# A lower rank for the third group in the tail, and four PSUM banks for each group

## The chip, the core and the metric

The kernel runs on one core of a Trainium2 chip. The metric is the time of the kernel on the device in microseconds, the median of several runs. The engines are TensorE (PE, the matrix engine), VectorE (DVE), ScalarE (ACT), GpSimd (POOL) and SyncE (SP, which here does nothing but start DMA transfers). All of them work through their own queue of instructions in the order in which the program puts them there, and wait for each other by semaphores.

## What is computed

Four layers work on a tensor x of 16 images, 32 channels and 128 by 128 pixels. Before each layer x is group-normalised, and its result is added to x.

```python
x = x + _L0_conv_ref(_gn(x), ...)   # a recurrent layer over the skewed rows, 128 steps
x = x + _L1_conv_ref(_gn(x), ...)   # a 3x3 layer of sums of absolute differences
x = x + _L2_conv_ref(_gn(x), ...)   # 2-D Hartley transform, 32x32 modes mixed over channels, and back
x = x + _L3_conv_ref(_gn(x), ...)   # five edge filters, each normalised, then a small U-net
```

The change concerns the end of the last two layers. Layer 2 transforms every image by two multiplications with a table of cosines and sines, keeps 32 by 32 modes, mixes the channels with one weight matrix for each mode, and transforms back. Layer 3 applies five edge filters with a mean and a variance for each image, and then this chain, in which every step needs all of the one before:

```python
y = conv3x3(y, conv1_w, conv1_b); y = maxpool2(y)      # 160 channels in, 128x128 pixels
y = conv3x3(y, conv2_w, conv2_b); y = maxpool2(y)      # 64x64
y = conv3x3(y, conv3_w, conv3_b); y = maxpool2(y)      # 32x32
y = conv3x3(y, conv4_w, conv4_b)                       # 16x16
y = deconv2x2(y, ...); y = conv3x3(y, conv5_w, ...)    # up to 32x32
y = deconv2x2(y, ...); y = conv3x3(y, conv6_w, ...)    # up to 64x64
y = deconv2x2(y, ...); y = conv3x3(y, conv7_w, ...)    # up to 128x128
return orig * y
```

## The kernel before

**Stages.** `stage0` computes layer 0 for all images. `rest` computes the other three. Its first part, `Differences.run`, computes layer 1 image by image, which takes most of the time; DVE and ACT form the differences, and PE sums them (L645). Layers 2 and 3 are computed by the class `After` for groups of four images: one image has 32 channels, so four fill the 128 partitions. There are four groups. While `Differences.run` works on the images of the next group, the work of a finished group is woven between its instructions. What is left when layer 1 has come to its last image is called the tail here: a part of the third group, and the whole fourth or last group, which needs the last image of layer 1.

**The stages of a group.** `forward` (L1028): loads `xh` of x2, transform by L1116, L1131 and L1088, a store of the modes to HBM and loads of them back in another layout; `mixing` with the weight tables `mix` (L1203); the result `z` goes through HBM. `back` (L1230): L1267 and L1312 transform back, DVE adds the result to x2 (L1290), takes its statistics (L1292) and SP stores x3. `statistics` (L1376): x3 comes in frames `xp` of 16 rows, ACT normalises them, and PE forms a Gram matrix of the frames (L1403), from which DVE gets the variances of the five filtered images (L1463) and with them one folded set of weights for conv1 (L1530, L1532). `conv1` (L1662): a small part for the left and right edges (L1693), then eight chunks of 16 rows, each 25 taps of 16 matmuls (L1721), with some more matmuls in the first and the last chunk (L1738). A chunk fills four PSUM accumulators, one for each image; DVE adds the edge parts (L1757) and takes the 2x2 maxima (L1645), and then DVE or ACT adds the bias and moves the result to its place (`spread`, L1656 and L1659). `small_layers` (L1544): conv2 to conv4 (L1568), and conv5 and conv6, each composed with its deconvolution (L902, L927). `last` (L1777): conv7 composed with its deconvolution, in eight rounds of four accumulators (L902, L927); after each round DVE scales the four (L1850) and multiplies them with x3 (L1813), and after each second round ACT adds the mean (L1823) and SP stores the output.

**The order of the work in the tail.** A `Weave` is a generator of a group's work. It yields after each small piece with the time that the piece is thought to take. `drain` (L453) runs two of them, one for what is left of the third group and one for the last group: it always steps the one whose own clock is behind. In this way the pieces of the two groups are traced in turns. The instructions of `stage0` and of layer 1 are pinned to the order in which they are traced (`keep_order`); those of the tail are not. There a scheduler at build time puts each engine's instructions in order: among those that are ready in its own model of the machine, it takes the one with the smallest priority number. This number comes from a counter, `tc.cur_priority`, which goes up as instructions are traced, so that before the change the priority is the order of tracing.

**Where the tiles lie.** PSUM has eight banks, and one accumulator is one bank. The pool `b_ps` with four banks belongs to groups 0 to 2 throughout. The pool `c_ps`, with the four banks that layer 1 leaves, belongs to the last group. An accumulator is taken by `acc` (L986):

```python
self.banks += 1
ps = self.spare if self.weave.alone and self.banks // 4 % 2 else self.ps
return ps.tile([128, 512], F32, name="acc")
```

`spare` of the last group is `b_ps`, and `alone` becomes true when the third group has ended: from then on the last group takes four accumulators from one pool and the next four from the other. In SBUF the third group's tiles are on the left, with two frames and two residual buffers `xr3` for `last`; the last group's are on the right, with four of each. `alone` has two more effects: `spread` then gives each second image to DVE and the others to ACT, whatever its caller asks for, and `last` plans its stores 4 us and not 14 us after ACT. `stretch` lengthens the planned waits of a weave.

Of the kernel before, what the change touches and what calls it, by code (L numbers as in the profile page):

```python
# [7 lines left out]
F32 = mybir.dt.float32  # L8
# [340 lines left out]
class Weave:  # L349
# [10 lines left out]
    def __init__(self, work):  # L360
        self.work, self.pending = work, None
        self.pe = self.dve = self.act = self.now = self.base = 0.0
        self.until = self.ready = 0.0
        self.draining = self.alone = False
        self.stretch = 1.0
        self.finished, self.count, self.put_off, self.for_act, self.ends = -1, 0, [], [], {}
# [42 lines left out]
    def step(self):  # L409
# [3 lines left out]
        if v is None:  # L413
            return None
        if v is SUMMED:
            wait = self.lag()
# [33 lines left out]
                self.pe = start + us * CLOCK  # L450


def drain(*weaves):  # L453

    live = list(weaves)
    for w in live:
        w.draining, w.stretch = True, 1.5
    while live:
        w = min(live, key=lambda w: w.now)
        us = w.step()  # L460
        w.now = max(w.now + (us or 0.0), w.until)
        w.due(float("inf") if us is None else w.now)
        if us is None:
            live.remove(w)
            for w in live:
                w.alone, w.stretch = True, 1.0


def keep_order(nc, tc, start):

    last = {}
    for i in nc.cur_bb.bb.instructions[start:]:
        if i.engine in last:
            tc.add_manual_dep(
                i,
                last[i.engine].name,
                mybir.DependencyInfo(mybir.DependencyClass.NoSync, mybir.DependencyReason.DATA),
                reason="order",
            )
        last[i.engine] = i  # L480
# [5 lines left out]
LATE = 1.5  # L486
SLACK, CLOCK = 3.0, 1.0
SUMMED = ("summed",)


def rest(nc, tc, cst, sel16, bias, m1, r1, a, d, out):


    with ExitStack() as ctx:
        sm = ctx.enter_context(tc.tile_pool(name="s1_sm", bufs=1))
        stat = sm.tile([128, B, 8, 6], F32, name="stat2")
        with tc.tile_pool(name="s1_ps0", bufs=2, space=PSUM) as ps:
            first = Differences(nc, sm, ps, cst, sel16, m1, r1, a["adder_w"], d, stat)
        bg = ctx.enter_context(tc.tile_pool(name="b_ps", bufs=4, space=PSUM))
        after = After(nc, tc, "left", sm, bg, cst, bias, a, d, stat, out)  # L500
        weave = after.weave = Weave(after.work(range(NG - 1)))
        start = len(nc.cur_bb.bb.instructions)
        with ExitStack() as front:
            first.run(tc, front, weave)
        keep_order(nc, tc, start)

        end = copy.copy(after)
        end.side, end.ps = "right", ctx.enter_context(tc.tile_pool(name="c_ps", bufs=4, space=PSUM))
        end.spare = bg

        end.buffers = {"t_x": 8, "xm": 8, "xw": 4, "t_w": 6, "t_r": 8, "frames": 4, "gm": 5, "e_v": 6, "l_x": 4}
        end.weave = Weave(end.work([NG - 1]))
        end.weave.now = end.weave.base = weave.now
        end.weave.finished = B - 1
        drain(weave, end.weave)


class Differences:
# [103 lines left out]
    def finish(self, b, half, acc, xr, **_):  # L622
        nc = self.nc
        v = [xr[k // 2][:, 512 * (k % 2) : 512 * (k % 2) + 512] for k in range(4)]
        for k in range(4):
            nc.vector.scalar_tensor_tensor(v[k], acc[k], self.sumw, v[k], ALU.subtract, ALU.add)
        for k in range(4):
            nc.vector.bn_stats(self.stat[:, b, 4 * half + k, :], v[k])

        def store():  # L630
            for i in range(2):
                by_rows(nc, xr[i], jc_rows(self.d["x2"], b, half, 8 * i, 8), True)
            if half:
                self.weave.finished = b

        start = max(self.weave.dve, self.weave.pe)
        self.weave.pe, self.weave.dve = start + 2.6, start + 5.6
        self.weave.later(max(self.weave.dve - self.weave.base, 0.0) + 0.5, store)

    def sums(self, acc, d, i, first, last):  # L640
        c = 1 if i % 3 == 1 else 0
        for k in range(4):
            for j in range(4):
                row = 16 * j + 4 * k
                self.nc.tensor.matmul(  # L645
                    acc[k][32 * j : 32 * j + 32, :],
                    self.sel16[:, i // 9, :],
                    d[:, row : row + 4, c : c + W],
                    start=first,
                    stop=last,  # L650
                )

    def linear(self, acc, q, tap):

        kh, kw = tap // 3, tap % 3
        for j in range(4):
            for k in range(4):
                rows = slice(32 * k, 32 * k + 32)
                row = 16 * j + 4 * k + kh
                self.nc.tensor.matmul(  # L660
                    acc[k][32 * j : 32 * j + 32, :],
                    self.sel16[rows, 8, :],
                    q[rows, row : row + 4, kw : kw + W],
                    start=False,
                    stop=False,
                )
        self.weave.pe = max(self.weave.pe, self.weave.now) + 0.45
# [110 lines left out]
def normalised(nc, pool, ps, weave, mv, n, avg, eps, out):  # L778
# [5 lines left out]
    nc.tensor.matmul(p[:, :n], avg, mean, start=True, stop=True)  # L784
    yield SUMMED
    nc.vector.tensor_copy(out[:, 0], p[:, :n])
# [6 lines left out]
    nc.tensor.matmul(p[:, :n], avg, v, start=True, stop=True)  # L793
    yield SUMMED
    nc.vector.tensor_copy(v, p[:, :n])
# [34 lines left out]
class Composed:  # L830
# [10 lines left out]
    def compose(self, pool, ps):  # L841
# [5 lines left out]
        for par in range(4):  # L847
            for tap in range(4):
# [6 lines left out]
                for i, (q, k) in enumerate(terms):  # L855
# [8 lines left out]
                    yield 0.4  # L864
        yield SUMMED
        t = pool.tile([128, 25, 32], F32, name="co_t")
# [9 lines left out]
        nc.vector.tensor_reduce(t[:, 24], w3.rearrange("p t o -> p o t"), AX.X, ALU.add)  # L876
        yield SUMMED
        nc.sync.dma_start(self.store, t.rearrange("p t o -> p (t o)"))
        p = ps.tile([128, 512], F32, name="acc")
        for j in range(4):  # L880
            nc.tensor.matmul(p[32 * j : 32 * j + 32, :1], t[:32, 24], self.bd[:32], start=True, stop=True)
        yield SUMMED
        nc.vector.tensor_add(self.bias, p[:, :1], self.b3)
# [72 lines left out]
class After:  # L956


    def __init__(self, nc, tc, side, sm, ps, cst, bias, a, d, stat, out):
        self.nc, self.tc, self.side, self.ps, self.cst, self.bias = nc, tc, side, ps, cst, bias  # L960
        self.a, self.d, self.stat, self.out = a, d, stat, out
        self.spare, self.banks = None, 0
        self.buffers = {"t_x": 4, "xm": 3, "xw": 2, "t_w": 3, "t_r": 4, "frames": 2, "gm": 3, "e_v": 3, "l_x": 2}
        store = [d["up"][i] for i in range(3)]
        self.up5 = Composed(nc, sm, a, "deconv1", "conv5", bias[:, 7:8], bias[:, 4:5], store[0])
        self.up6 = Composed(nc, sm, a, "deconv2", "conv6", bias[:, 8:9], bias[:, 5:6], store[1])
        self.up7 = Composed(nc, sm, a, "deconv3", "conv7", bias[:, 9:10], bias[:, 6:7], store[2])
# [17 lines left out]

    def acc(self):  # L986

        self.banks += 1
        ps = self.spare if self.weave.alone and self.banks // 4 % 2 else self.ps
        return ps.tile([128, 512], F32, name="acc")  # L990

    def prepare(self):

# [998 lines left out]
def program(nc, tc, a, at, out):  # L1992
    def scratch(name, *shape):
        return nc.dram_tensor(name, shape, F32, kind="Internal").ap()

    d = {f"x{i}": scratch(f"x{i}_d", B, C, H, W) for i in (1, 2, 3)}
    d["q"] = nc.dram_tensor("q_d", (B, C, H + 2, W + 2), F16, kind="Internal").ap()
    d["xm"], d["z"] = (scratch(n, B, C, M1, M1) for n in ("xm_d", "z_d"))
    d["y6"] = scratch("y6_d", NG, 128, 66 * 66)
    d["fold"] = scratch("fold_d", 5, 128, 90 * 32)  # L2000
    d["up"] = scratch("up_d", 3, 128, 25 * 32)
    with tc.tile_pool(name="keep", bufs=1) as keep:
        cw = keep.tile(list(a["consts"].shape), F32, name="cw")
        nc.scalar.dma_start(cw, a["consts"])
        cst = {n: cw[:, lo:hi] for n, (lo, hi) in at.items()}
        sel16 = keep.tile([128, 9, 32], F16, name="sel16")
        nc.scalar.dma_start(sel16, a["sel16"])
        bias = keep.tile([128, 10], F32, name="bias")
        nc.scalar.dma_start(bias, a["bias"])

        m1, r1 = stage0(nc, tc, keep, cst, a["x"], a["xs"], a["w0"], a["b1"], a["b2"], d["x1"])
        rest(nc, tc, cst, sel16, bias, m1, r1, a, d, out)
# [17 lines left out]
```

## Time and profile before

| | us |
|---|---|
| median of 3 runs | 6794.93 |
| lowest and highest of them | 6793.73, 6800.52 |
| the profiled execution | 6791.52 |
| its span, first to last instruction | 6789.7 |
| PE busy in the span | 5402.1 (80%) |
| DVE busy | 5640.5 (83%) |
| ACT busy | 5537.1 (82%) |

The shares of the whole span belong to layer 1 and say little about the tail. The page shows the tail at the right end of the rows that cut the span into 40 slices: DVE and ACT fall from nine tenths to two or three, while PE stays at seven to nine.

```profile
PE   3697777787777879997877788999877774897896
DVE  7898999999999999989999999999999993224223
ACT  3898999999999999999999999999999991132222
PEclk9998999999999989998989899999889996997997
```

A digit is the busy share of one fortieth of the span (170 us) in tenths; in the row PEclk it is the clock that TensorE was granted, in tenths of the full speed. Line numbers in the profile are those of the kernel before; the changed kernel's lines lie up to three further down or up.

### The profile page before, as it was taken

The numbers are of one execution on the slowest core, as the hardware profiler recorded it, in microseconds if no ns is written. First come the engines' busy times: TensorE is split into PE (matmuls) and PEld (weight loads), VectorE is DVE, ScalarE is ACT, GpSimd is POOL, SyncE is SP. The second block draws the span as 40 slices with busy tenths as digits, with TensorE's granted clock in tenths as the row PEclk, the third lists the DMA queues.
The fourth block names the chain that finished last, engine by engine and source line by source line (L and its number), as shares of the span: only waits on it lengthen the run. The fifth ranks groups of instructions, "written<-read, shape, count | busy, mean of one in ns | idle before, by whom it ended". The sixth has DMA issues, their size and how long they took to land. (4 is left out here: it accounts for less than half of the span.)

```text
span 6789.7 us, 271989 instructions
## 1 busy us (share of the span) xinstructions
PE 5402.1 (80%) x127580; PEld 2816.8 (41%) x127580; DVE 5640.5 (83%) x6946; ACT 5537.1 (82%) x3419; POOL 90.9 (1%) x83
## 2 busy tenths in 40 slices
PE   3697777787777879997877788999877774897896
PEld 3575333333343433333334343333333343454564
DVE  7898999999999999989999999999999993224223
ACT  3898999999999999999999999999999991132222
POOL 0000000000000010000000000000000000000000
PEclk9998999999999989998989899999889996997997
DMA  7553312213343431312353443222264246342414
GB/s 316 201 189 126 77 49 63 60 30 71 80 127 108 113 109 46 85 44 59 86 152 92 145 117 79 56 57 51 61 139 120 66 135 194 99 149 72 92 42 104
DMA packets 381685, 689.12 MB, mean 101 GB/s; under 512 B 68048, under 2 KB 234448, under 8 KB 369680
## 3 DMA queue, kind: packets, MB, share of 16 engines
q1 hardware_dynamic: 373088, 637.30, 34.2%
q0 software_dynamic: 7040, 33.80, 1.5%
q8 instruction: 998, 16.35, 1.0%
q14 instruction: 127, 1.04, 0.1%
q10 hardware_dynamic: 432, 0.64, 0.0%
HBM read 507.28 MB, written 164.32 MB: 99 GB/s over the span
## 5 line engine op out<-in xcount | busy, mean ns | idle before, releaser
L755 ACT ACTIVATE d_act<-q,neg 128x8192 f16<-128x8192 f16 (+1 forms) x622 | 4404.3, 7148 | 138.0 <-PE acc L645 117.2
L758 DVE TENSOR_SCALAR d_dve<-q,qw 128x8192 f16<-128x8192 f16 (+1 forms) x1682 | 3878.9, 2363 | 163.5 <-PE acc L645 143.3
L645 PE MATMUL acc<-d_dve,sel 128*32 128x512 f16 x26912 | 1864.5, 400 | 475.4 <-DVE d_dve L758 412.2
L645 PEld LDWEIGHTS <-sel 128*32 128x32 f16 x36864 | 1014.3, 100 | 2122.4 <-issue 1455.1
L1721 PE MATMUL acc<-xp,wf 32*32 32x512 f32 x25600 | 1040.4, 616 | 57.4 <-issue 53.3
L645 PE MATMUL acc<-d_act,sel 128*32 128x512 f16 x9952 | 716.4, 408 | 329.6 <-ACT d_act L755 310.0
L1721 PEld LDWEIGHTS acc<-xp,wf 32*32 32x32 f32 x25600 | 416.1, 104 | 429.0 <-issue 345.8
L1659 ACT ACTIVATE y<-pooled,b 32x128 f32<-32x128 f32 x488 | 195.1, 400 | 389.1 <-DVE pooled L1645 382.4
L675 PE MATMUL acc<-q,zero 128*32 128x512 f16 x7088 | 509.2, 399 | 0.0
L902 PE MATMUL acc<-y,u_conv 32*32 32x256 f32 (+1 forms) x9728 | 373.8, 472 | 90.8 <-issue 63.7
L221 PE MATMUL pg<-h,wb 64*64 64x20 f32 (+15 forms) x8192 | 340.1, 303 | 61.5 <-DVE h L249 35.3
L235 ACT ACTIVATE gt<-pg,bias 128x20 f32<-128x20 f32 (+15 forms) x1024 | 332.5, 384 | 42.3 <-PE pg L221 40.4
L1362 ACT ACTIVATE xp<-xp,shift,stats 128x1280 f32<-128x1280 f32 (+1 forms) x128 | 182.6, 1434 | 185.8 <-DMA xp<-x_d 170.6
L221 PEld LDWEIGHTS pg<-h,wb 64*64 64x64 f32 x8192 | 250.1, 149 | 136.9 <-DVE h L249 82.5
L675 PEld LDWEIGHTS <-zero 128*32 128x32 f16 x7088 | 214.7, 101 | 195.7 <-issue 40.2
L1850 DVE TENSOR_SCALAR s<-acc,l_ms,l_one 128x512 f32<-128x512 f32 x128 | 102.1, 821 | 202.8 <-PE acc L902 202.8
L902 PEld LDWEIGHTS acc<-y,u_conv 32*32 32x32 f32 x9728 | 177.0, 111 | 216.4 <-issue 164.2
L1823 ACT ACTIVATE xr<-xr,l_ms 128x1024 f32<-128x1024 f32 x64 | 70.0, 1141 | 222.8 <-DVE xr L1813 222.8
L1403 PE MATMUL acc<-xp 32*64 32x204 f32 (+3 forms) x8576 | 238.6, 344 | 16.1 <-issue 15.6
L1403 PEld LDWEIGHTS acc<-xp 32*64 32x64 f32 (+1 forms) x8576 | 168.2, 135 | 108.9 <-issue 100.4
L221 PE MATMUL pg<-xn,wb 64*64 64x2 f32 (+63 forms) x4096 | 184.1, 289 | 28.6 <-issue 18.6
L1568 PE MATMUL acc<-y,w_conv 32*32 32x512 f32 (+2 forms) x4608 | 162.5, 497 | 28.4 <-issue 16.5
(218 smaller groups left out, 3711.9 us busy)
## 6 DMA issues: line engine op xcount, KB each, us to landing
xp<-x_d SPq DMA_DIRECT2D x112, 640.0 KB
q<-q_d SPq DMA_DIRECT2D x128, 536.2 KB
xr<-x_d SPq DMA_DIRECT2D x128, 512.0 KB
x_in<-in_x_dram SPq DMA_DIRECT2D x16, 2048.0 KB
xn<-in_xs_dram SPq DMA_DIRECT2D x64, 512.0 KB
res<-in_x_dram SPq DMA_DIRECT2D x64, 512.0 KB
x_d<-res SPq DMA_DIRECT2D x64, 512.0 KB
xq<-x_d SPq DMA_DIRECT2D x256, 128.0 KB
```

The lines of the kernel that those rows point to most:

```text
L221: nc.tensor.matmul(bank[c][q][64 * pair : 64 * pair + 64, :, :width], wb[half, 4 * kind + KIND[q]].rearrange("p b o -> p (b o)"), v[half], ...
L235: nc.scalar.activation(gt[:, q, :, :n], bank[c][q][:, :, :n], AF.Tanh if q == G else AF.Sigmoid, bias=bias[:, KIND[q] : KIND[q] + 1],)
L645: self.nc.tensor.matmul(acc[k][32 * j : 32 * j + 32, :], self.sel16[:, i // 9, :], d[:, row : row + 4, c : c + W], start=first, stop=last,)
L675: self.nc.tensor.matmul(acc[k][32 * j : 32 * j + 32, :], self.zero, q[:, :4, :W], start=False, stop=False)
L755: nc.scalar.activation(dst, src, AF.Relu, bias=self.neg[:, i : i + 1])
L758: nc.vector.tensor_scalar(dst, src, self.qw[:, i : i + 1], 0.0, ALU.subtract, ALU.max)
L902: nc.tensor.matmul(acc[blk][32 * j : 32 * j + 32, o : o + rows * n], t[part, 4 * par + tap, :], src[part, top : top + rows, left : left + ...
L1362: nc.scalar.activation(v, v, AF.Identity, bias=self.shift3, scale=self.stats3[:, 1])
L1403: nc.tensor.matmul(gram[blk][j : j + width, at : at + n], xp[part, l, 2 + j : 2 + j + width], xp[part, rows, j : j + width + 4], start=sta ...
L1568: nc.tensor.matmul(acc[blk][32 * j : 32 * j + 32, : rows * n], wc[name][part, tap, :], src[part, at : at + rows, kw : kw + n], start=tap == 0,
L1659: nc.scalar.activation(d, s, AF.Identity, bias=bj)
L1721: nc.tensor.matmul(acc[blk][32 * j : 32 * j + 32, :], tap_of("all", tap)[rows], xp[rows, 4 * j + kh : 4 * j + kh + 4, kw : kw + W], start= ...
```

## The change

```diff
-def drain(*weaves):
-
-    live = list(weaves)
-    for w in live:
-        w.draining, w.stretch = True, 1.5
+def drain(tc, *weaves):
+
+    live, turn = list(weaves), {}
+    for k, w in enumerate(live):
+        w.draining, w.alone, w.stretch = True, True, 1.5
+        turn[w] = tc.cur_priority + BEHIND * (len(live) - k)
     while live:
         w = min(live, key=lambda w: w.now)
+        tc.cur_priority = turn[w]
         us = w.step()
         w.now = max(w.now + (us or 0.0), w.until)
         w.due(float("inf") if us is None else w.now)
+        turn[w] = tc.cur_priority
         if us is None:
             live.remove(w)
-            for w in live:
-                w.alone, w.stretch = True, 1.0
+            for v in live:
+                v.stretch = 1.0
...
+BEHIND = 1000000
...
         end.side, end.ps = "right", ctx.enter_context(tc.tile_pool(name="c_ps", bufs=4, space=PSUM))
-        end.spare = bg
...
-        drain(weave, end.weave)
+        drain(tc, weave, end.weave)
...
-        self.spare, self.banks = None, 0
...
     def acc(self):
 
-        self.banks += 1
-        ps = self.spare if self.weave.alone and self.banks // 4 % 2 else self.ps
-        return ps.tile([128, 512], F32, name="acc")
+        return self.ps.tile([128, 512], F32, name="acc")
```

Each of the two weaves gets a counter of priorities of its own. The third group's (the first argument of `drain`) starts two million above the present value, the last group's one million above, so that every instruction of the last group in the tail has a smaller number than every one of the third. The weaves are still stepped by their clocks, so the tracing takes turns as before. Each group has its own four PSUM banks to the end. `alone` is true for both groups throughout the tail, and with it the division of `spread` between DVE and ACT; `stretch` becomes 1.0 for the group that is left when the other's tracing has ended.

## The prediction

> **What bounds the kernel now.** The change touches only the tail, so I first looked for where the tail begins. The view of the sums of stage 1 (L645) shows its last matmul at 5592.9 us; the span is 6789.7 us, so the tail is 1196.8 us. Then I cut the tail into stretches:
>
> ```profile
> core 0: us, PE busy (x) PEld busy (x) DVE busy (x) ACT busy (x) POOL busy (x), PEclk, DMA share, GB/s
> 5593.00:5740.00 147.00, 72.71 (x1746) 53.44 (x1738) 67.54 (x217) 27.14 (x43) 5.32 (x11) 0.72 0.75 221
> 5740.00:6253.00 513.00, 435.72 (x14185) 249.06 (x14186) 162.07 (x471) 117.79 (x248) 8.82 (x19) 0.89 0.36 107
> 6253.00:6519.00 266.00, 229.01 (x7194) 142.17 (x7192) 69.45 (x138) 69.80 (x129) 0.21 (x1) 0.94 0.38 87
> 6519.00:6592.60 73.60, 73.51 (x2363) 62.03 (x2367) 11.13 (x40) 6.40 (x16) 0.00 (x0) 1.00 0.02 4
> 6592.60:6636.00 43.40, 36.45 (x1153) 24.58 (x1146) 20.20 (x76) 13.29 (x36) 0.00 (x0) 0.87 0.11 29
> 6636.00:6703.00 67.00, 45.37 (x1207) 27.28 (x1207) 23.28 (x40) 17.14 (x29) 0.00 (x0) 0.65 0.62 134
> 6703.00:6770.70 67.70, 46.83 (x2027) 33.04 (x2027) 33.70 (x49) 13.47 (x12) 0.00 (x0) 0.90 0.43 97
> ```
>
> TensorE (PE) is the engine that matters; DVE and ACT are busy for a third of the time or less. Each fp32 matmul of the program leaves two records, which I call passes. Up to 6519 us two groups share PE, and it makes 14185 passes in 513 us and 7194 in 266 us: 36 to 37 ns each, waits included. From 6519 us the last group is alone: in its first convolution 2363 passes in 73.6 us, 31.1 ns each at full clock. Behind that PE is idle a third of the time, at clocks down to 0.65.
>
> The sources of single lines, next, say when the last group passes each stage, in the order mode weights, back transform, Gram matrix, normalisation:
>
> ```profile
> L1088 PE MATMUL acc<-cw,t x64: 267/276/402, 5664.0 to 5700.3; 128*128 128x32 f32 x64
> L1203 PE MATMUL acc<-xs,mix x1024: 176/195/223, 5740.2 to 5806.8; 128*32 128x8 f32 x171
> L1267 PE MATMUL acc<-cw,zi x1024: 184/191/256, 5818.2 to 5892.4; 32*32 32x32 f32 x171
> L1312 PE MATMUL acc<-cw,o x256: 269/270/372, 5900.0 to 6004.2; 32*128 32x128 f32 x128
> L1403 PE MATMUL acc<-xp x2144: 188/331/383, 6053.2 to 6166.1; 32*64 32x204 f32 x181, 32*32 32x72 f32 x6, 32*32 32x36 f32 x5, 32*64 32x68 f32 x2
> L1693 PE MATMUL acc<-sides,wf x640: 209/236/259, 6222.5 to 6252.1; 32*32 32x32 f32 x160
> ```
>
> So the last group needs 660 us (5593 to 6253) to reach its first convolution, because it stands in PE's queue between the third group's matmuls. Third, the timeline of DVE, for the price of emptying four accumulators after a chunk of conv1 and after a round of the last layer:
>
> ```profile
> 6592.60 0.44 DVE L1757 TENSOR_TENSOR acc<-acc,cut 128x4 f32<-128x4 f32 x4 [23.09 <-PE acc L1721]
> 6593.08 1.29 DVE L1645 TENSOR_REDUCE pooled<-acc 128x128 f32<-128x512 f32 x2
> 6594.28 0.43 DVE L1757 TENSOR_TENSOR acc<-acc,cut 128x4 f32<-128x4 f32 x4
> 6594.75 1.29 DVE L1645 TENSOR_REDUCE pooled<-acc 128x128 f32<-128x512 f32 x2
> ...
> 6705.49 1.53 DVE L1850 TENSOR_SCALAR s<-acc,l_ms,l_one 128x512 f32<-128x512 f32 x2 [10.89 <-PE acc L902]
> 6706.94 0.74 DVE L1813 SCALAR_TENSOR_TENSOR xr<-xr,l_ms,s 128x512 f32<-128x512 f32 x1
> 6707.59 0.81 DVE L1850 TENSOR_SCALAR s<-acc,l_ms,l_one 128x512 f32<-128x512 f32 x1
> 6708.31 0.74 DVE L1813 SCALAR_TENSOR_TENSOR xr<-xr,l_ms,s 128x512 f32<-128x512 f32 x1
> 6708.97 0.82 DVE L1850 TENSOR_SCALAR s<-acc,l_ms,l_one 128x512 f32<-128x512 f32 x1
> ```
>
> The last of four banks is free 3.4 us after a chunk and 4.3 us after a round. With eight banks PE is in the other four meanwhile and does not feel it.
>
> **What the Trainium skill says.** "TensorE: Matmul & The Clock Gate", section "Step-by-step: what each phase is for": matmuls run in program order, only weight loads are pulled ahead. The trace agrees: the last group's statistics were ready for their matmul (L784) at 6008.3 us, it ran at 6020.1, behind third-group matmuls. Same page, "Why this matters for your kernels": PE gaps above about 3 us bring the half clock. It agrees: 1.00 in the dense stretch, 0.65 between 6636 and 6703. "TensorEngine Tiling (Array Packing)", section "PSUM Bottleneck": tiling speeds TensorE up, not the emptying of PSUM. It agrees, by the 3.4 and 4.3 us.
>
> **The change part by part.**
>
> 1. *Priority.* Priority decides the order in which instructions are put on each engine at build time, and the order of the changed program shows what comes of it. The last group's matmuls stand in unbroken stages; third-group matmuls come only between, 5 to 160 at a time. Behind the very last matmul of the last group stand 5490 third-group matmuls (10980 passes), 3129 of them conv1. In before, some 3370 matmuls (6750 passes) stand alone at the end, those of the stretches from 6519 us. So the overlap of two groups shrinks by 2100 matmuls.
>
> The last group on its own, on before's time axis. Forward transform: its loads no longer wait on SP and its statistics on DVE behind third-group frames; the eight loads of x2 were issued some 3.3 us apart, from 5599.7, so it ends near 5643 (was 5701). From there to the weights 39 us as before, waiting for DMA: 5682. Weights, 1024 passes: dense windows of small matmuls in before reach some 380 passes in 10 us (6240 to 6250), so 27 ns each, 28 us: 5710. The trip through HBM 11 us, as before (5806.8 to 5818.2): 5721. L1267: 28 us by the same rate; three of its four blocks now stand one after the other, with 4 array tiles of 16 in use, and two evictions: 38 us, 5759. 8 us to L1312 as before. L1312: 16 rounds of 2.6 us on DVE, with reloads: 48 us, 5815. Normalisation and first frame 19 us (49 before, 30 of it behind third-group matmuls): 5834. Gram 2144 passes, 28 ns: 60 us, 5894. Gram tables and folded weights, DVE and DMA, 49 us (56 before): 5943. L1693 704 passes at 27 ns and eviction: 23 us, 5966. That is 287 us earlier than before.
>
> 2. *No extra banks.* conv1 is 6736 passes with its edges, at 31.1 ns 210 us, and at each of 8 chunks PE waits 3.4 us plus some 1 us to drain and refill: 36 us. 6212. The third group fills at most 2 us of such a wait. conv2 to conv4 43.4 us and 3 for conv2's second round: 6259. Up-sampling and last layer 134 us (6636 to 6770), plus 5 for the second round of up6, plus 16: a round took 10.3 us (starts of L1850 at 6705.5, 6715.2, 6726.6) and will take some 12. 6414.
>
> Then the third group: 6594 passes of conv1, 205 us, and 36 us of waits: 6655. 47 us: 6702. 155 us, and 6 because it has only two residual buffers (on SP the reload for unit 3 stands behind a store of unit 2): 6863. From the last matmul to the end 19 us as before: 6882.
>
> 3. *Clock.* Each of the 16 waits at a chunk can leave a stretch at half clock, where a pass takes twice as long (maximum 1058 ns in L902 beside a median of 398, in L1721 1058 beside 595). No stretch of before shows this in conv1 alone; bounds are 0 and 16 times 2 us. I take 15.
>
> 4. *Half of the bias steps on DVE for both groups* (alone is set for both), and later steps traced with stretch 1.5: DVE is 33% busy in the tail; 2.3 us per chunk come behind the pooling, so nothing waits. Cost nothing; if that cover went, 2.3 us in 16 chunks. The last group's SP, POOL, DVE and ACT instructions also pass the third group's; what that delays is third-group filler.
>
> Sum: 6882 + 15 = 6897, 107 us above the span of 6789.7. The profiled run took 6791.5 us, the median is 6794.9; 6794.9 + 107 = 6902, rounded to **6900**.
>
> **Rivals.** *Forecast*, 0.75, 6900: two groups in series overlap less than two interleaved.
>
> *More stalls*, 0.15, 7010: stretches alone go cold. If the clock stays near 0.65 to 0.87 as in 6592 to 6703 in both last layers, and fillers of the third group hold up the last group in the queues (a gram matmul in front of a weight matmul waiting for its frame), some 110 us are added. For: before's own alone stretches. Against: conv1 ran at 1.00.
>
> *Faster*, 0.06, 6765: the last group's chain is all latency, and its stalls go. Floors: 5936 at conv1, 2 us for each chunk, no loss by four banks: 6162, 6340 at its last matmul, then 205+16+178+19 for the third group: 6758 span. The deciding point: what follows the last group costs at least 205+43+134+19 = 401 us, so the last group must be done by 6388. My sum says 6414, and then the third group's waits must vanish too.
>
> *It does not do what it says*, 0.04, 6795: stages just change places and the sum of waits stays. The built order speaks against it.
>
> **How the numbers follow.** 6900 is the likeliest. Its own range is 6830 to 6985: the chain to conv1 30 us either way, bank waits 2 to 6 us in place of 4.5, clock 0 to 32. Two parts in ten lie outside, mostly at the upper rival, so the range is 6830 to 6990. The three runs of before lie within 0.1%, so 0.2% (14 us) is what can be told from no change. Faster 0.06, same 0.04, slower 0.90.
>
> **What would show it.** L1403 of the last group near 5834 and its conv1 near 5970 to 6210, dense but for 4 us gaps; the third group's conv1 from about 6414, alone on PE; waits of L1721 for DVE's pooling, which before hardly has (1.2 us); the span's end on the third group. I am wrong if the last group's final matmul comes before 6388, if conv1's chunks follow each other without gaps on four banks, or if PE stands still behind filler for tens of us.

## The result, and the profile after

| | median, us | runs |
|---|---|---|
| before | 6797.73 | 4 |
| after | 6889.17 | 4 |

The ratio is 1.0134, with a 95% interval of 1.0117 to 1.0152: the change costs 91 us. The profiled execution took 6879.81 us, its span is 6878.0.

The windows of after are cut at the stages of the tail. Stage 1 ended at 5585.2 us in this execution, 8 us earlier than in that of before, so stretches are compared by their length. Columns as in the windows of before.

```profile
core 0: us, PE busy (x) PEld busy (x) DVE busy (x) ACT busy (x) POOL busy (x), PEclk, DMA share, GB/s
5585.00:5936.00 351.00, 219.60 (x6832) 172.12 (x6840) 133.85 (x387) 67.70 (x115) 9.03 (x20) 0.69 0.67 202
5936.00:6184.00 248.00, 243.15 (x7114) 167.76 (x7082) 71.29 (x228) 38.00 (x84) 5.02 (x10) 0.96 0.18 50
6184.00:6236.00 52.00, 44.91 (x1511) 30.03 (x1513) 20.38 (x76) 13.72 (x37) 0.00 (x0) 0.86 0.10 26
6236.00:6394.00 158.00, 122.08 (x3465) 73.67 (x3474) 57.56 (x92) 30.12 (x40) 0.00 (x0) 0.69 0.45 98
6394.00:6642.00 248.00, 235.89 (x6594) 153.42 (x6574) 44.31 (x152) 47.84 (x97) 0.21 (x1) 0.94 0.17 43
6642.00:6693.00 51.00, 40.17 (x1152) 24.66 (x1152) 19.71 (x72) 13.17 (x35) 0.00 (x0) 0.83 0.10 25
6693.00:6863.00 170.00, 127.26 (x3234) 80.95 (x3234) 61.65 (x94) 33.84 (x45) 0.00 (x0) 0.65 0.41 91
```

The rows are, in order: the last group's way to its first convolution, its conv1, its conv2 to conv4, its up-sampling and last layer; then conv1, conv2 to conv4 and up-sampling of the third group. The last group's own share is 6736, 1152 and 3234 passes in rows two to four. So row four holds only 231 passes of the third group, and 10980 passes stand behind the last group's end. The two groups run one after the other.

A cut of before after the same 351 us shows where the loss begins (PE is busy for 68% of it, so the tail's first part isn't at the seven to nine tenths of its later parts):

```profile
5593.20:5944.20 351.00, 239.68 (x7922) 151.86 (x7919) 107.74 (x316) 56.30 (x109) 5.53 (x12) 0.82 0.50 148
```

Now the whole account can be done. In its first 351 us after makes 1090 passes fewer than before. Before needs 826.5 us for the 21953 passes from there to its last matmul, 37.65 ns each. At this price the missing passes are some 41 us. In after the last group's conv1, with third-group passes in its gaps, runs at 248/7114 = 34.9 ns a pass, which wins 20 us; its small layers and rounds take 210/4976 = 42.2 ns, which loses 23; the third group alone takes 469/10980 = 42.7 ns, which loses 56. The sum is 100 us to the last matmul. From there to the end after takes 15 us and before 19. The spans from the end of stage 1 differ by 1292.8 - 1196.5 = 96 us. The median loss, 91 us, is smaller, as these are two single executions.

The single lines of after, in the 351 us to the last group's conv1, answer to those of before:

```profile
L1088 PE MATMUL acc<-cw,t x64: 194/276/297, 5608.2 to 5630.4; 128*128 128x32 f32 x64
L1203 PE MATMUL acc<-xs,mix x1024: 190/201/223, 5666.4 to 5696.0; 128*32 128x8 f32 x171
L1267 PE MATMUL acc<-cw,zi x1024: 204/236/259, 5706.7 to 5742.5; 32*32 32x32 f32 x171
L1312 PE MATMUL acc<-cw,o x256: 416/416/577, 5745.4 to 5792.3; 32*128 32x128 f32 x128
L1693 PE MATMUL acc<-sides,wf x640: 209/238/259, 5915.6 to 5931.6; 32*32 32x32 f32 x160
```

A stage now takes about as long as its own matmuls or its own evictions need. L1267 went from 74 us to 36, L1312 from 104 to 47. But what stands beside them is small. The windows of PE over L1312, first in after and then in before (columns: PE busy and passes, PEclk, DMA share, GB/s):

```profile
5745.00:5793.00 48.00, 47.56 (x348) 0.50 0.75 252
```

```profile
5900.00:6004.00 104.00, 100.06 (x2427) 1.00 0.64 194
```

PE is busy in both by its records, but a pass costs 138 ns in after and 43 in before. In after the filler comes in turns of 2 to 12 passes, Gram matmuls of the third group between L1312 matmuls, which have another tile shape (32*64 against 32*128):

```profile
5760.23 0.94 PE L1403 MATMUL acc<-xp 32*64 32x204 f32 x4
5761.10 2.66 PE L1312 MATMUL acc<-cw,o 32*128 32x128 f32 x16
5763.69 0.97 PE L1403 MATMUL acc<-xp 32*64 32x204 f32 x12
```

A turn of 4 passes takes as long as one of 12. So the missing passes are not only idle time of PE.

What four banks do at the border of two chunks is seen in windows of 2 us (same columns), in the third group's lone conv1:

```profile
6452.00:6454.00 2.00, 2.00 (x73) 1.00 0.03 8
6454.00:6456.00 2.00, 1.02 (x15) 1.00 0.24 54
6456.00:6458.00 2.00, 2.00 (x29) 0.83 1.10 307
6458.00:6460.00 2.00, 2.00 (x41) 0.50 1.16 282
6460.00:6462.00 2.00, 2.00 (x59) 0.82 0.09 20
6462.00:6464.00 2.00, 2.00 (x84) 1.00 0.00 0
```

A window counts every pass that runs in it, so a pass across the border of two windows counts twice; in windows as short as these that matters, as a pass lasts some 0.6 us. Counted by their starts, the four windows from 6454 hold 2, 27, 28 and 46 passes, 103 in all; at 31.1 ns a pass 257 would fit. The missing 154 are 4.8 us. PE stands still for only 1 us of it, by its records. The rest has two parts. DVE empties the banks one after the other, and the last is free 3.4 us after the chunk's end, as in before. And the clock was 0.50 for 3.4 us (6457.3 to 6460.7), after 3 us in which PE began only 17 passes. If half of the passes are lost at half clock, 1.7 of the 4.8 us are the clock's and some 3.1 the banks', by this estimate.

### The profile page after: what moved, and what is told of

It is laid out like the page before. It is cut to its first block, busy times and chain, and to the rows that moved or that the text cites. A ratio compares the mean times of both kernels' runs of the same rounds, so it can differ in the third digit from the quotient of the medians.

```text
span 6878.0 us, 272010 instructions
## 1 busy us (share of the span) xinstructions
PE 5520.6 (80%) x127580; PEld 2936.2 (43%) x127580; DVE 5657.6 (82%) x7010; ACT 5512.2 (80%) x3355; POOL 87.2 (1%) x83
## 5 line engine op out<-in xcount | busy, mean ns | idle before, releaser
L1721 PE MATMUL acc<-xp,wf 32*32 32x512 f32 x25600 | 992.1, 617 | 33.5 <-issue 18.2
L1721 PEld LDWEIGHTS acc<-xp,wf 32*32 32x32 f32 x25600 | 463.6, 104 | 415.7 <-issue 297.5
L1659 ACT ACTIVATE y<-pooled,b 32x128 f32<-32x128 f32 x384 | 153.6, 400 | 432.8 <-DVE pooled L1645 427.8
L905 PE MATMUL acc<-y,u_conv 32*32 32x256 f32 (+1 forms) x9728 | 396.3, 516 | 106.0 <-issue 63.7
L1757 DVE TENSOR_TENSOR acc<-acc,cut 128x4 f32<-128x4 f32 x256 | 35.3, 165 | 373.8 <-PE acc L1721 371.6
L221 PEld LDWEIGHTS pg<-h,wb 64*64 64x64 f32 x8192 | 252.8, 151 | 134.7 <-DVE h L249 79.6
L1403 PE MATMUL acc<-xp 32*64 32x204 f32 (+3 forms) x8576 | 256.6, 356 | 60.4 <-ACT xp L1368 30.9
L905 PEld LDWEIGHTS acc<-y,u_conv 32*32 32x32 f32 x9728 | 192.2, 118 | 253.0 <-issue 153.0
L1403 PEld LDWEIGHTS acc<-xp 32*64 32x64 f32 (+1 forms) x8576 | 180.5, 140 | 131.8 <-issue 90.6
```

The costliest lines, as they stand in the source:

```text
L221: nc.tensor.matmul(bank[c][q][64 * pair : 64 * pair + 64, :, :width], wb[half, 4 * kind + KIND[q]].rearrange("p b o -> p (b o)"), v[half], ...
L905: nc.tensor.matmul(acc[blk][32 * j : 32 * j + 32, o : o + rows * n], t[part, 4 * par + tap, :], src[part, top : top + rows, left : left + ...
L1403: nc.tensor.matmul(gram[blk][j : j + width, at : at + n], xp[part, l, 2 + j : 2 + j + width], xp[part, rows, j : j + width + 4], start=sta ...
L1659: nc.scalar.activation(d, s, AF.Identity, bias=bj)
L1721: nc.tensor.matmul(acc[blk][32 * j : 32 * j + 32, :], tap_of("all", tap)[rows], xp[rows, 4 * j + kh : 4 * j + kh + 4, kw : kw + W], start= ...
```

## The experiments

All ratios are to the kernel before, on the same chip in the same batch.

| run | what it is | us | ratio, 95% interval |
|---|---|---|---|
| e1_banks | before, no spare banks | 6836.52 | 1.0066, 1.0042 to 1.0089 |
| e2_norank | after without the rank | 6827.48 | 1.0053, 1.0032 to 1.0075 |
| e3_eight | after, spare banks for the third group, too early | 6886.1 | 1.0140, 1.0119 to 1.0160 |
| e3b_eight | the same, from its conv1 on | 6827.5 | 1.0043, 1.0028 to 1.0059 |
| e4_stage | before, rank that changes by stage | 6863.55 | 1.0100, 1.0074 to 1.0127 |
| e5_b2000 | after, ranks 2,000 apart | 6947.74 | 1.0222, 1.0198 to 1.0245 |
| e5_b0 | after, ranks 0 apart | 9079.01 | 1.3354, 1.3320 to 1.3388 |
| e6_reverse | after, ranks exchanged | 6924.85 | 1.0183, 1.0160 to 1.0206 |
| e7_lead150 | before, last group 150 us ahead | 6793.43 | 1.0009, 1.0001 to 1.0018 |
| e7_lead300 | before, last group 300 us ahead | 6813.77 | 1.0045, 1.0031 to 1.0059 |
| e8_grain3 | before, turns at least 3 us long | 6798.75 | 1.0008, 0.9999 to 1.0018 |
| e8_grain8 | before, turns at least 8 us long | 6827.38 | 1.0047, 1.0034 to 1.0059 |

### One half of the change at a time

The banks alone, in before:

```diff
-        self.banks += 1
-        ps = self.spare if self.weave.alone and self.banks // 4 % 2 else self.ps
-        return ps.tile([128, 512], F32, name="acc")
+        return self.ps.tile([128, 512], F32, name="acc")
```

> The kernel before, with the last group held to its own four PSUM banks to the end; order and rank as before. Series theory (most of the loss is lost overlap of the two groups, and four banks cost only where a group is alone): before is alone only from about 6519 us, so it loses 3 chunk gaps of 4.5 us, 7 us in conv2 to conv4 and 24 us in the up-sampling and last layer: about 6842 us. Bank theory (the missing banks are the loss, rank matters little): most of the 91 us is here, about 6880 us.

The rank taken out of after, which leaves its banks and its division of the bias steps:

```diff
-        turn[w] = tc.cur_priority + BEHIND * (len(live) - k)
...
-        tc.cur_priority = turn[w]
...
-        turn[w] = tc.cur_priority
```

> The changed kernel without the ranks: both groups share one counter of priorities, four banks each, bias steps divided between DVE and ACT for both groups. Series theory: the same as e1_banks within 15 us, about 6840 us, as the division of the bias steps costs nothing; so the rank on its own is worth about +50 us. Bank theory: about 6885 us, so the rank is worth nothing. If the division of the bias steps matters, this differs from e1_banks by more than 15 us.

The two agree within their intervals: 1.0066 and 1.0053. The windows of e1_banks show the price where the last group is alone, conv2 to conv4 and then the rounds:

```profile
6602.00:6651.00 49.00, 43.06 (x1152) 26.49 (x1152) 19.71 (x74) 12.88 (x34) 0.00 (x0) 0.84 0.10 26
6651.00:6810.00 159.00, 119.31 (x3234) 70.01 (x3234) 57.80 (x90) 30.78 (x43) 0.00 (x0) 0.69 0.44 98
```

The same passes took 43.4 and 134.7 us in before: 30 us of 41 are lost here, the others in the end of conv1. So the banks cost 32 to 41 us with the old order, and from e2_norank to after the rank adds 0.8%, some 55 us. As the two runs agree, the division of the bias steps costs nothing that these runs can tell.

### The banks with the new order

In after the lone group is the third. It got the last group's banks when that had ended. For this the last group is written down first (the ranks make its instructions first anyhow), and `acc` alternates only after a flag:

```diff
-        w = min(live, key=lambda w: w.now)
+        w = live[-1]
...
+        after.spare = end.ps
...
+        self.banks += 1
+        ps = self.spare if self.spare and self.weave.wide and self.banks // 4 % 2 else self.ps
+        return ps.tile([128, 512], F32, name="acc")
...
+            weave.wide = weave.wide or ch == 1
```

> The changed kernel, with the last group traced first and the third group given both pools of banks, eight in all, from its second chunk of conv1 on; ranks as in the change. Series theory: the third group alone wins back its waits, 7 chunks of 4.5 us and about 35 us in the later layers, some 65 us: about 6825 us, still 25 to 30 us above the kernel before. Bank theory: all of the loss goes, 6800 us or less.

It missed. The flag belongs to the weave of groups 0 to 2 and was still set by an earlier group. So the third group took banks of `c_ps` even for its Gram tables and edge parts, and those waited for the last group's end: its edge parts ran from 6446.5 to 6465.5 us, where after had done them by 6245. What was won by eight banks (some 70 us by its stages) went there. With the flag reset at the tail's start:

```diff
-        w.draining, w.alone, w.stretch = True, True, 1.5
+        w.draining, w.alone, w.wide, w.stretch = True, True, False, 1.5
```

> The changed kernel with the last group written first in the trace and its four banks handed to the third group, which alternates both pools only from its own first convolution on (the flag starts false in the tail). If the third group's lone stretch is held by the four banks (eight matmul runs of convolution 1 with 4.5 us waits, 13 us instead of 10 us per round of up-sampling), it loses about 65 us, as seen in the third group's conv1 to end of the run before (222 + 44 + 133 us against 248 + 52 + 170): 6825 us. If that stretch was short only because of what was late before it, the time stays at 6885 us. Deciding point 6855.

6827.5 us: as the bank theory said. The windows of e3b_eight over the third group's conv1, conv2 to conv4, and rounds:

```profile
6409.00:6629.00 220.00, 214.42 (x6620) 159.57 (x6625) 44.56 (x152) 47.86 (x97) 0.21 (x1) 1.00 0.19 49
6629.00:6672.00 43.00, 32.91 (x1151) 24.33 (x1119) 19.83 (x74) 13.21 (x35) 0.00 (x0) 0.83 0.11 30
6672.00:6809.00 137.00, 91.00 (x3234) 57.92 (x3234) 57.76 (x89) 30.62 (x42) 0.00 (x0) 0.76 0.49 113
```

400 us in place of 469, and the clock in conv1 is 1.00 in place of 0.94. At the border of two chunks the windows of 2 us show no half clock, though the next frame is loaded there in both runs (DMA share above 1):

```profile
6470.00:6472.00 2.00, 2.00 (x76) 1.00 1.17 304
6472.00:6474.00 2.00, 1.64 (x56) 1.00 0.32 77
6474.00:6476.00 2.00, 2.00 (x69) 1.00 0.00 0
6476.00:6478.00 2.00, 2.00 (x82) 1.00 0.00 0
```

So with the rank in place the four banks of the lone third group are worth some 62 us of the 91. The other 29 (1.0043) are what the rank costs when the lone group keeps eight banks. This agrees with the account above: 41 - 20 + 23 for the earlier rows, and 36.3 ns a pass in place of 37.65 for the lone 11005, -14, sum 30. The banks cost more with the new order than with the old because the lone stretch grew from 6750 passes to 10980. The edit has a side effect: as the last group is traced first, all of the third group is traced with `stretch` 1.0. That this alone moves nothing was not tried; up to the last group's end the two kernels differ by 2 us (809 in after, 811 in e3b_eight).

### Is it the order of the ranks?

```diff
-        turn[w] = tc.cur_priority + BEHIND * (len(live) - k)
+        turn[w] = tc.cur_priority + BEHIND * (1 + k)
```

> The changed kernel with the ranks exchanged: the third group's instructions come first, the last group's are the filler. If a full rank costs because it puts the groups in series, whichever goes first, the last group's convolution, small layers and rounds stand alone at the end and the time is as in the changed kernel, 6870 to 6890 us. If the cost lies in ranking the group with the long chain first (its 350 us from the end of stage 1 to its convolution are only half filled), the third group's dense work covers that chain here: third group 5590 to about 6230, then Gram rest 75, tables and weights 55, convolution 248, 50, 165 and 15 of the last group alone: about 6835 us. Deciding point 6855.

6925 us, above both values; the theory that ranking the group with the long chain first is to blame doesn't hold. The third group's dense work does cover the first 351 us (8401 passes, more than the 7922 of before). But the last group, as filler, came too slowly, and when the third group had ended it still had inverse transform, Gram matrix and tables before it, with nothing beside them:

```profile
6245.00:6302.00 57.00, 21.51 (x133) 19.80 (x132) 32.33 (x72) 3.50 (x4) 2.60 (x5) 0.50 0.91 281
6302.00:6442.00 140.00, 70.26 (x2875) 61.92 (x2889) 40.24 (x133) 41.70 (x74) 5.80 (x13) 0.72 0.55 164
```

3008 passes in 197 us are 65 ns each. A full rank costs in either direction, but at different places: with the last group first its chain is poorly filled, with the third group first it is left over. The lone group has four banks here too, so the 6925 us are not the price of the rank alone; the reversed order with eight banks was not run.

### Can a smaller advance win?

First a rank that changes by stage, in before: third group to its conv1, then the last group to its conv1, then the third group's backlog, then both by one counter.

```diff
+    turn = {k: tc.cur_priority + BEHIND * k for k in range(4)}
...
+        rank = 3 if weaves[1].dense else 1 if w is weaves[1] else 0 if not weaves[0].dense else 2
+        tc.cur_priority = turn[rank]
         us = w.step()
+        turn[rank] = tc.cur_priority
...
+        weave.dense = True
```

> The kernel before with its eight banks, but ranks by stage: first the third group until its conv1 begins, then the last group until its conv1 begins, then the third group's remaining work, then both in turns. Series theory: the last group's chain to conv1 is shortened as in the change while the third group's conv1 fills its gaps, and both groups then overlap until the last one's own end: about 6730 us, 65 us below the kernel before. A theory that ranking costs in itself (fillers hold up the queues): 6800 us or more.

It missed: slower by 1%. While the last group went through weights to Gram tables, the third group's conv1 was ready as filler the whole time, and yet PE was busy 69%; before, over the third group's conv1 and the same stages, shows what interleaving by steps makes (first line e4_stage, second before):

```profile
5771.00:6063.00 292.00, 201.95 (x6639) 148.31 (x6635) 98.10 (x260) 52.31 (x97) 8.61 (x18) 0.68 0.51 158
```

```profile
5790.00:6090.00 300.00, 272.82 (x8255) 154.21 (x8252) 80.21 (x224) 84.28 (x186) 6.47 (x14) 0.98 0.45 133
```

44.0 ns a pass against 36.3. PE's order is fixed at build time, so a ranked-down group stands only where the scheduler's own model foresees a hole. That the model's holes are smaller than the real ones would explain the idle time; this is argued, not tried. Idle time isn't all of it: in e4_stage, too, PE is busy from 5845 to 5895 us by its records and makes 341 passes there at a clock of 0.50, short turns of conv1 between the matmuls of the back transform.

Then the ranks of after with less distance between them (`BEHIND` 2,000 or 0 in place of 1,000,000), so that the groups' numbers overlap from some point on:

> The changed kernel with the constant at 2,000 instead of 1,000,000: the last group leads by 2,000 numbers only, so its chain up to its first convolution still goes ahead of the third group, but from there both groups' convolutions, small layers and rounds interleave. Theory A (what costs is that small layers and rounds run with one group's banks alone): 350 us to the last group's convolution as in the changed kernel, 14,400 passes of convolution at 32 ns = 461, 8,900 passes of small layers and rounds at 37 ns = 330, 15 for the end, 1156 after 5590: about 6750 us, faster than before. Theory B (pulling the last group's chain forward is what costs, later work runs at the 38.8 ns a pass that the kernel before has after 5940 us): 23,300 passes x 38.8 ns = 904 after 5940, 6845 us. Deciding point 6800.

> The constant at 0: both groups count from the same number at the tail's start, so neither leads in count of instructions; the third group's rounds lie beside the last group's convolution as in the kernel before, and only the last group's rounds (1,750 matmuls) stand alone at the end, against 3,375 lone matmuls in the kernel before. Theory A: 26,600 passes at 38 ns = 1010, 160 for the lone rounds, 15 for the end, 1185 after 5590: about 6775 us. Theory B (any lead of the last group over the order of the kernel before costs): above the 6827 us of the kernel with four banks and no rank. Deciding point 6800.

Both missed by far, and both theories with them: I had thought only of how far one group leads, not of how finely they alternate. With a counter for each group, equal numbers make the scheduler take one or two matmuls from each in turn. Counted in the built order of TensorE, the tail changes from one group's stage to another's 398 times in before, 139 in after, but 6119 times in e5_b2000 and 7911 in e5_b0. The timeline of PE in e5_b0, where the third group's conv1 (L1721) meets the last group's Gram matrix (L1403), and then before at the same meeting (start, length, passes):

```profile
6998.80 1.92 PE L1721 MATMUL acc<-xp,wf 32*32 32x512 f32 x4
7000.65 0.94 PE L1403 MATMUL acc<-xp 32*64 32x204 f32 x4
7001.52 1.92 PE L1721 MATMUL acc<-xp,wf 32*32 32x512 f32 x4
7003.37 0.94 PE L1403 MATMUL acc<-xp 32*64 32x204 f32 x2
```

```profile
6100.65 1.20 PE L1721 MATMUL acc<-xp,wf 32*32 32x512 f32 x32
6101.77 0.95 PE L1403 MATMUL acc<-xp 32*64 32x204 f32 x32
6102.65 1.20 PE L1721 MATMUL acc<-xp,wf 32*32 32x512 f32 x32
```

A turn of two or four passes takes 0.9 to 1.9 us here; a turn of 32 takes 1.0 to 1.2 us in before, whose window from 6100 to 6120 us has 678 passes, 30 ns each. The window of this meeting in e5_b0:

```profile
6362.00:8177.00 1815.00, 1814.40 (x4268) 333.38 (x4272) 23.33 (x101) 56.87 (x113) 1.36 (x4) 0.50 0.03 10
```

425 ns a pass, at half clock for 1.8 ms, although PE is busy all the time by its records. Alternation by itself is not the reason. In e5_b2000 both groups' conv1, with tiles of one shape, alternate by one or two matmuls through both of these windows (columns: PE busy and passes, PEclk, DMA share, GB/s):

```profile
6290.00:6390.00 100.00, 99.92 (x2908) 1.00 0.07 17
6390.00:6490.00 100.00, 98.90 (x1812) 1.00 0.05 14
```

The first runs at 34 ns a pass, about as fast as whole steps, the second at 55. The built order of e5_b2000 shows a difference: each matmul has a place in the array, its tile, and in the first window none of the 1444 pairs of neighbours in PE's order stand on the same tile; from 6400 to 6480 us 334 of 718 pairs do. In e5_b0 from 6900 to 7000 us only 3 of 101 pairs of neighbours share a part of the array, but 74 change the tile shape. So the meeting of two shapes goes with the high price there, and the meeting on one tile with the smaller one; a run with one of them changed alone was not made.

So a lead has to be given with whole steps kept, in the tracing and with one counter. In before, with a lead of 150 or 300 us, and banks for whichever group is left:

```diff
-        w = min(live, key=lambda w: w.now)
+        w = min(live, key=lambda w: w.now - LEAD * (w is weaves[-1]))
...
-        end.spare = bg
+        end.spare, after.spare = bg, end.ps
```

> The kernel before with one edit to how the two groups' steps are written down: the last group is taken whenever its clock stands less than 150 us ahead of the third group's (before: whenever it is behind), and whichever group is left alone may use both pools. One counter numbers all, so work still alternates in whole steps of 16 matmuls or more. The lone matmuls at the end go from 3,375 to about 2,000. If a lead by itself is harmless and only the full rank and the one-by-one alternation cost, the third group's small layers and rounds cover what stood alone: 6770 us. If pulling the last group's chain forward costs as such: 6820 us or more. Deciding point 6795.

> The same with a lead of 300 us: both groups' convolutions overlap over their whole length, both end nearly together, and only some 900 matmuls stand alone. Harmless lead: 6755 us. A lead that costs by itself: above the run with 150 us, 6840 us or more.

150 us change next to nothing (1.0009), 300 cost 0.45%. A lead isn't harmless. The windows of the first 351 us from the end of stage 1, with a lead of 150 us and then of 300:

```profile
5596.50:5947.50 351.00, 234.70 (x7114) 164.79 (x7120) 132.03 (x386) 59.01 (x112) 11.23 (x23) 0.73 0.61 189
5594.70:5945.70 351.00, 223.70 (x6682) 156.97 (x6678) 129.97 (x387) 57.79 (x100) 11.66 (x25) 0.69 0.66 200
```

Before makes 7922 passes in this time, after 6832. That the early stages are short of work to put beside the last group's chain, so that pulling the chain into them widens the holes, would explain it; this was not tried alone. By the totals, what is lost there comes back at the end with 150 us, and with 300 it doesn't.

### Do the changes of group cost in before?

```diff
-        w = min(live, key=lambda w: w.now)
+        w = min(live, key=lambda v: v.now - GRAIN * (v is w))
```

> The kernel before with one edit: the group that was written down last keeps its turn until its clock is 3 us ahead of the other's. The order of the stages, the banks and the lone end stay as they are, but on TensorE the tail changes from one group to the other 146 times instead of 398. In the kernel before, 16 passes of convolution 1 between Gram stretches take 0.77 us against 0.50 at 31.1 ns a pass, and 32 Gram passes 0.95 against 0.86 at 27 ns: about 0.19 us a change of group. If each change of group costs that: 252 x 0.19 = 48 us less, 6740 us (the kernels of the same batch before at about 6790). If the price is one of the one-by-one alternation of the count-0 kernel only, and changes every 16 matmuls are hidden: no change, within 10 us. Deciding point 6768.

> The same with 8 us: 95 changes of group. If changes cost 0.19 us each: 303 x 0.19 = 58 us less, 6732 us, unless the longer stretches make each group wait for its evictions and its chain (8 us against waits of 4.5 us per chunk): then above the run with 3 us. If changes cost nothing: no change or slower.

With 146 changes in place of 398 the time is the same, so at 16 matmuls or more a change of group isn't on the path. With turns of 8 us it is 0.47% slower; by the stages the third group's conv1 ends 12 us later than in before (541 us against 529 from the end of stage 1) and the last group's 25 us later (1024 against 999). Why isn't settled: longer waits for an eviction or the chain would fit. No version tried beats before.

## Why the prediction was right

6900 was forecast, 6889 came. Its steps by their lengths, the first from the end of stage 1:

| step | predicted, us | measured |
|---|---|---|
| last group to its first L1721 | 373 | 350 |
| its conv1 | 246 | 248 |
| conv2 to conv4 | 47 | 51 |
| up-sampling and last layer | 155 | 158 |
| third group's conv1 | 241 | 248 |
| conv2 to conv4 | 47 | 52 |
| up-sampling and last layer | 161 | 170 |
| to the end | 19 | 15 |
| half clock, as a sum | 15 | in the rows above |

The total is better than its terms. The chain was forecast 23 us too long and the half clock is a term of 15 us without a row of its own, while the other steps were 26 us too short in sum. That these errors cancel to 12 us is luck; the order of the stages and the size of most terms are not.

*Priority.* Right: stages unbroken, and the 10980 passes behind the last group are those of the built order. The chain was 23 us too long. The forecast priced three stretches from rows of before that still held other waits: Gram tables and folded weights took 35 us and not 49, normalisation 12 and not 19, L1312 began 3 us after L1267 and not 8. In the other direction, the Gram matrix took 76 us and not 60: PE waited for frames (14 us for ACT's L1368). The remaining steps were some 13 us shorter than forecast.

*Banks.* Right in place and nearly in size, but not in its parts. The forecast had 4.5 us of waiting for each chunk, and 1 us for the clock. A border in the third group's conv1 costs 4.8 us in all, of which by the estimate above some 3.1 are the banks' and 1.7 the clock's. In sum the two conv1 take 38 and 43 us more than their passes at 31.1 ns; the forecast had 36 for each and 15 for both. Of the third group's later waits, 3 and 21 us were put down to the banks, so 60 in all with conv1; e3b_eight gives 62. The 6 us for two residual buffers are not borne out: e3b_eight has the same two, and its rounds take 137 us against 134.7 of the last group in before. The waits of L1721 for DVE's pooling are there, 12.8 us in 14 waits, where before had 1.2.

*Clock.* Right that each border can leave a half clock, and somewhat too small: the clock stood at 0.50 for 19.5 us of the last group's conv1 and for 27.3 us of the third group's. Half of that, an estimate of the loss, is 23 us where the forecast took 15 and its bound was 32. One of the two pairs of durations behind "twice as long" mixes shapes: L902's median of 398 ns is that of passes of 256 columns, and its longest one has 512. L1721's 1058 beside 595 compares like with like and is 1.8 times.

*The reason.* The forecast said that two groups in series overlap less than two interleaved. By the runs this is one of three parts: some 29 us for the rank when the lone group has eight banks, 32 to 41 us for four banks in the old order (e2_norank and e1_banks), and the 20 to 30 that are left because the rank lengthens the stretch that has four banks. No part alone explains 91 us. The forecast's sum had all three, its sentence only the first.

*Rivals.* *Faster* had its deciding point at 6388 us for the last group's end. It came at 6394 in an execution whose stage 1 ended 8 us earlier, so at 6402 on before's axis, and the third group then needed 469 us where that rival had 399 (205 + 16 + 178). *More stalls* was right on the clock (0.65 to 0.69 in both last layers) but not on its price. What it said of the queues happened too, and it is also one of the forecast's signs of being wrong, PE standing still behind filler for tens of us:

```profile
5663.55 2.32 PE L1403 MATMUL acc<-xp 32*64 32x204 f32 x40 [24.37 <-ACT xp L1368]
```

For 24 us PE stood before a Gram matmul of the third group whose frame had not come. Most of it cost the last group nothing, because its weights came by DMA only at some 5655 us; L1203, which stood behind the filler, began at 5666.4, so some 9 us of its chain may be this wait. *It does not do what it says* is excluded by the windows.

## What to carry to other kernels

Before giving one of two independent streams the higher rank, count what is left alone at the end, and price that stretch with the buffers that it will have: here the change cost 91 us with four PSUM banks for the lone group and 29 with eight. A strict rank needs enough filler for the ranked chain, in the scheduler's order and not only in the program; in the kernel before, turns of whole steps took less time than every rank tried. And if two streams get counters of their own, see that their numbers don't overlap: alternation by single matmuls of two tile shapes was the most expensive order of all.

## What the runs showed of the hardware that I had not expected

A short turn of matmuls of one tile shape, between turns of another, is nearly as dear as a long one. In e5_b0 a Gram turn of two or four passes lasts 0.87 us and a conv1 turn of four 1.85 us, each from its start to the next turn's, at a clock of 0.50; in before turns of 32 passes last 0.88 and 1.12 us at a clock of 1.00. With the half clock taken out, by an estimate 0.44 and 0.93 us, one or two matmuls still need half or more of the time of sixteen. That makes 425 ns a pass against 30. The Trainium skill ("TensorE: Matmul & The Clock Gate", section "The mechanism") says that matmuls on different tiles of the array overlap; before's trace agrees with its 30 ns, and so does e5_b2000 with its 34 ns where neighbours stand on different tiles. E5_b0 shows an order in which they don't. In both kernels a turn begins, by the records, only as the turn of the other shape before it ends, though in e5_b0 the tiles of neighbours are nearly always different ones; in before sixteen matmuls of a turn share this time, in e5_b0 one or two. In e5_b0 the clock stood at 0.50 for 1815 us with PE busy throughout by its records, so a busy PE isn't a PE at speed. Why shape matters was not tried.

In after a stop of 1.0 to 1.3 us at a chunk's border was followed by 3.4 us or more at half clock, at all seven borders of the third group's conv1. The same page, section "A second HAM failure mode: psum-queue depth-cycling", tells of short idle times between groups of matmuls that make the clock swing when a kernel cycles through PSUM banks. The trace of after agrees: it falls to 0.50 at the border. So the gaps above about 3 us of which the prediction speaks are not needed for the half clock. But the stop alone doesn't bring it either. With eight banks e3b_eight keeps 1.00 in all of the third group's conv1, with four stops of 0.7 to 1.1 us in it; behind them PE is dense at once, with 39 passes or more in the poorest 3 us, where the border at 6454 us in after has 14. The low rate isn't the whole rule: e3b_eight has 11 passes in 3 us at its first border and no half clock. What sets it stays open.
